# Two graph layers on one core: layer 0's attention with stationary values, two heads in the array's column halves, separate sums spread by transfers, and masks kept in DRAM

## Chip, cores and metric

One core of one Trainium2 chip. The metric is device microseconds of one execution; a kernel's runs here agree within 0.4%. The kernel before takes 5757.45 us (median of 3 runs, 5756.26 to 5758.06).

Ratios are the mean time of one kernel's runs over the mean of the other's runs of the same rounds, with a 95% interval. They are therefore not quite the ratio of the medians quoted.

## The reference, cut to what matters

Eight batches of 2048 nodes with 256 features go through two layers. Layer 0 is attention with four heads of 64 features. Its softmax is taken separately over each chunk of 256 keys, and the eight chunks' results are added:

```python
q, k, v = ...                                     # (B, H=4, N=2048, Dh=64)
kc = k.reshape(B, H, Nc, CHUNK, Dh)               # Nc = 8 chunks of CHUNK = 256 keys
vc = v.reshape(B, H, Nc, CHUNK, Dh)
scores = jnp.einsum('bhnd,bhjcd->bhnjc', q, kc) / jnp.sqrt(Dh)
scores = jnp.clip(scores, -10.0, 10.0)
scores = jnp.where(mask == 0, -10.0, scores)      # mask: the adjacency matrix
attn = jax.nn.softmax(scores, axis=-1)            # within a chunk
ctx = jnp.einsum('bhnjc,bhjcd->bhnd', attn, vc)   # and summed over the chunks
out = layernorm(ctx @ Wo.T + bo + x) * gamma + beta
```

So there are 8 chunks x 4 heads = 32 sums for every query, and a numerator must be divided by its own chunk's sum before it is added to the others. Layer 1 is a graph attention over the same adjacency matrix; the change touches only where it gets its mask.

## The kernel before: what the change and the argument touch

A batch's queries are worked on in four blocks of 512. The logits stand with keys on partitions. The mask is folded into the upper bound of the clip (`bound`, int8, resident in SBUF).

```python
def logits(pool, q, k, p, nb, mt):                # one key tile, two heads
    s = ps_s()
    for i in range(2):
        nc.tensor.matmul(s[:, i, :], k[p][i*DH:(i+1)*DH, mt*P:(mt+1)*P],
                         q[p][i*DH:(i+1)*DH, cols], start=True, stop=True)      # L219
    e = pool.tile([P, 2, NB], F32, tag="e", name="e", bufs=2 * KT)
    nc.vector.scalar_tensor_tensor(e, s, -CLIP * SC, bound[...], op0=ALU.max, op1=ALU.min)   # L224
    nc.scalar.activation(e, e, AF.Exp, scale=1.0 / SC)                          # L228
    return e

def mix(pool, es, ctx4, p, j):                    # one chunk, two heads
    for t2 in range(TB // 2):
        a = ps_a()[:, 0:4 * (DH + 1)].rearrange("p (s d) -> p s d", s=4)
        for s in range(4):
            t, i = 2 * t2 + s // 2, s % 2
            for kt in range(KT):
                nc.tensor.matmul(                                               # L238
                    a[:, s, :], es[kt][:, i, t*P:(t+1)*P], v[:, j*KT+kt, 2*p+i, :],  # v ends in a column of ones
                    start=kt == 0, stop=kt == KT - 1)
        rz = small.tile([P, 4], F32, tag="rz", name="rz")
        nc.vector.reciprocal(rz, a[:, :, DH])                                   # L243
        # DVE: a * rz into ctx4 or part (L248, L251); POOL: ctx4 += part (L252)

for nb in range(NNB):                             # a block
    for p, j in todo:
        es = [logits(...) for kt in range(KT)]
        if ahead is not None: mix(...)            # the chunk before
    ...
    finish_layer0(pool, xs[nb], rns[nb], ctx4)    # transposes L262, projection L271, norm
    start_layer1(xs[nb], nb, sd)                  # norm, transposes L183, projection L300
```

## Time and profile before

The lines that show what bounds this kernel are in the prediction. Layer 0's attention is measured in one batch from the first logits to the last multiplication with values; its tail from there to layer 1's first multiplication (L352).

| kernel before | us |
|---|---|
| one batch (period) | 710.0 |
| attention, 797.9 to 1275.8 | 477.9, of which TensorE busy 468.5 |
| tail, 1275.8 to 1328.5 | 52.7 |
| one block, L300 to L300 | 116.3, of which TensorE busy 110.85 |

The table of windows gives that block as follows. After the window and its length come the busy us (with the number of instructions) of PE, PEld, DVE, ACT and POOL, then the granted TensorE clock, the share of the DMA engines and GB/s.

```profile
1083.30:1199.60 116.30, 110.85 (x690) 82.43 (x690) 66.97 (x139) 40.95 (x45) 32.13 (x37) 0.93 0.00 1
```

### The profile page before, as it was taken

Reading aid. Unit: us, or ns where it says so; the run is one execution under the profiler, and the core shown is the slowest. Engines: PE = TensorE matmul, PEld = TensorE weight load, DVE = VectorE, ACT = ScalarE, POOL = GpSimd, SP = SyncE. Lnnn points to the kernel's source line nnn. Section 1 sums busy time; section 2 is a strip of 40 time slices with the busy share of each in tenths; the row PEclk is TensorE's granted clock in tenths of the full one; section 3 lists DMA queues with packets and bytes.
Section 4 is the critical chain, followed back from the end, with each engine's and each line's share of the span. In section 5 each row is a group of like instructions: output and inputs, shape, how many; then the busy total and the mean of one; then the engine's idle time right before and its main releaser. Section 6 shows DMA issues by size and latency. Waiting matters only on the chain.

```text
span 5753.9 us, 73951 instructions
## 1 busy us (share of the span) xinstructions
PE 5208.2 (91%) x29840; PEld 3939.6 (68%) x29840; DVE 3477.6 (60%) x6501; ACT 2191.4 (38%) x2545; POOL 1228.1 (21%) x1369
## 2 busy tenths in 40 slices
PE   7999799987999889998899978999789997899978
PEld 4777667766677666776667757676576776767767
DVE  4555755558455584555845558455584555845567
ACT  3333443334433344333533335433353333533334
POOL 2222102231022301223112221123211232112221
PEclk7999899999999899998999989999899988999889
DMA  4000000000000000000000000000000000000000
GB/s 150 1 1 1 15 15 1 1 1 15 15 1 1 1 15 15 1 1 1 19 11 1 1 1 23 8 1 1 1 23 8 1 1 1 23 4 1 1 1 15
DMA packets 39203, 57.16 MB, mean 10 GB/s; under 512 B 2000, under 2 KB 36816, under 8 KB 36816
## 3 DMA queue, kind: packets, MB, share of 16 engines
q1 hardware_dynamic: 38864, 52.44, 2.8%
q8 instruction: 238, 3.90, 0.3%
q14 instruction: 101, 0.83, 0.0%
HBM read 35.65 MB, written 16.78 MB: 9 GB/s over the span
## 4 chain that ended last, share of the span: by engine, by line
PE 74%; DVE 14%; POOL 6%; ACT 4%; issue 2%; DMA 0%; POOLq 0%; SPq 0%; ACTq 0%; DVEq 0%
PE ps_a L238 32%; PE ps_s L219 17%; PE ps_a L352 10%; PE ps_m L194 4%; DVE d L328 3%; PE ps_m L300 3%; DVE e L343 2%; DVE st L331 2%; PE ps_m L203 2%; PE ps_m L183 2%; PE ps_s L346 2%; POOL o L282 1%; DVE e L224 1%; PE ps_m L271 1%; ACT e L341 1%
## 5 line engine op out<-in xcount | busy, mean ns | idle before, releaser
L238 PEld LDWEIGHTS ps_a<-v,e 128*128 128x128 f32 x16384 | 1994.8, 202 | 357.8 <-issue 321.4
L238 PE MATMUL ps_a<-v,e 128*128 128x65 f32 x16384 | 2061.0, 287 | 0.0
L228 ACT ACTIVATE e<-e 128x1024 f32<-128x1024 f32 x1024 | 1081.8, 1056 | 1682.4 <-DVE e L224 1650.2
L224 DVE SCALAR_TENSOR_TENSOR e<-ps_s,bound 128x1024 f32<-128x1024 f32 x1024 | 1213.4, 1217 | 273.4 <-PE ps_s L219 273.2
L219 PE MATMUL ps_s<-q,k 64*128 64x512 f32 x4096 | 1211.3, 638 | 66.3 <-DVE e L224 66.3
L252 POOL TENSOR_TENSOR ctx<-ctx,part 128x256 f32<-128x256 f32 x896 | 648.0, 723 | 2698.9 <-DVE part L251 2698.9
L352 PE MATMUL ps_a<-g,eT 128*128 128x257 f32 x4096 | 952.9, 385 | 66.9 <-ACT eT L348 45.9
L352 PEld LDWEIGHTS ps_a<-g,eT 128*128 128x128 f32 x4096 | 756.7, 190 | 214.0 <-ACT eT L348 83.5
L219 PEld LDWEIGHTS ps_s<-q,k 64*128 64x128 f32 x4096 | 389.6, 190 | 391.2 <-issue 148.8
L243 DVE RECIPROCAL rz<-ps_a 128x4 f32<-128x4 f32 x1024 | 182.7, 180 | 783.3 <-PE ps_a L238 783.3
L346 PE MATMUL ps_s<-ident,e 128*128 128x128 f32 x2048 | 288.0, 282 | 180.7 <-DVE e L343 179.8
L251 DVE TENSOR_TENSOR part<-ps_a,rz 128x256 f32<-128x256 f32 x896 | 379.6, 424 | 88.5 <-DVE rz L243 1.4
L360 POOL TENSOR_TENSOR x<-x,r 128x256 f32<-128x256 f32 x128 | 136.3, 1065 | 1254.8 <-DVE st L332 511.9
L346 PEld LDWEIGHTS ps_s<-ident,e 128*128 128x128 f32 x2048 | 247.4, 145 | 221.7 <-DVE e L343 114.4
L348 ACT ACTIVATE eT<-ps_s 128x512 f32<-128x512 f32 x256 | 150.6, 590 | 615.8 <-PE ps_s L346 575.2
L343 DVE TENSOR_TENSOR e<-e,e 128x1024 f32<-128x1024 f32 x256 | 310.1, 1217 | 79.3 <-ACT e L342 79.3
L341 ACT ACTIVATE e<-d,st 128x1024 f32<-128x1024 f32 x256 | 291.2, 1137 | 112.8 <-DVE st L334 112.8
L328 DVE SCALAR_TENSOR_TENSOR d<-sign,dst 128x2048 f32<-128x2048 int8 x128 | 312.7, 2448 | 9.6 <-ACT dst L324 9.6
L342 ACT ACTIVATE e<-d,st 128x1024 f32<-128x1024 f32 x256 | 291.1, 1137 | 0.0
L331 DVE TENSOR_REDUCE st<-d 128x1 f32<-128x2048 f32 x128 | 290.5, 2274 | 0.0
L183 PE MATMUL ps_m<-ident,hn 128*128 128x128 f32 x512 | 121.0, 368 | 165.7 <-ACT hn L173 165.2
L183 PEld LDWEIGHTS ps_m<-ident,hn 128*128 128x128 f32 x512 | 67.2, 175 | 288.8 <-ACT hn L173 237.5
(71 smaller groups left out, 3130.3 us busy)
## 6 DMA issues: line engine op xcount, KB each, us to landing
rows<-in_adj_dram SPq DMA_DIRECT2D x16, 1024.0 KB, 5.0
x<-in_x_dram SPq DMA_DIRECT2D x32, 512.0 KB, 3.8
out_dram<-x SPq DMA_DIRECT2D x32, 512.0 KB, 2.9
raw<-in_L_gnn_Wq_dram SPq DMA_DIRECT2D x1, 256.0 KB, 4.7
raw<-in_L_gnn_Wk_dram SPq DMA_DIRECT2D x1, 256.0 KB, 4.9
raw<-in_L_gnn_Wv_dram SPq DMA_DIRECT2D x1, 256.0 KB, 5.3
raw<-in_L_gnn_Wo_dram SPq DMA_DIRECT2D x1, 256.0 KB, 5.1
w1s<-in_L_gnn_W_dram SPq DMA_DIRECT2D x1, 256.0 KB, 6.4
```

Source lines behind the costliest of these rows:

```text
L219: nc.tensor.matmul(s[:, i, :], k[p][i * DH:(i + 1) * DH, mt * P:(mt + 1) * P], q[p][i * DH:(i + 1) * DH, cols], start=True, stop=True,)
L224: nc.vector.scalar_tensor_tensor(e, s, -CLIP * SC, bound[:, mt, cols][:, None, :].to_broadcast([P, 2, NB]), op0=ALU.max, op1=ALU.min,)
L228: nc.scalar.activation(e, e, AF.Exp, scale=1.0 / SC)
L238: nc.tensor.matmul(a[:, s, :], es[kt][:, i, t * P:(t + 1) * P], v[:, j * KT + kt, 2 * p + i, :], start=kt == 0, stop=kt == KT - 1,)
L251: nc.vector.tensor_tensor(part, num, rzb, op=ALU.mult)
L252: nc.gpsimd.tensor_tensor(dst, dst, part, op=ALU.add)
L328: nc.vector.scalar_tensor_tensor(d, sign[:, t, :], BIG, dst, op0=ALU.mult, op1=ALU.min)
L331: nc.vector.tensor_reduce(dmax, d, AX.X, ALU.max)
L341: nc.scalar.activation(e1, d[:, cols], AF.Exp, bias=b1)
L343: nc.vector.tensor_tensor(e1, e1, e2, op=ALU.max)
L346: nc.tensor.transpose(pt[:, k * P:(k + 1) * P], e1[:, k * P:(k + 1) * P], ident)
L352: nc.tensor.matmul(acc, eT[:, k * P:(k + 1) * P], g[:, m, :], start=m == 0, stop=m == NT - 1)
```

## The change

The intent is to take load and passes off TensorE. Instead of the exponentials, the values are stationary (64 columns), and the exponentials stream in 512 columns. Two heads then use the two column halves of the array. The result now stands with features on partitions, so a sum per query can't be applied as a scalar per partition. The sums come from matmuls of their own against a tile of ones (`picks`, four heads in four column quarters), are inverted once per half block, written to DRAM and spread over 64 partitions per head by broadcasting transfers. The unnormalised numerators wait for that in SBUF tiles `au` of 8 KB per partition, for which room is made by moving both masks to DRAM. The finish of a block is put inside the next block's loop.

```diff
-    bound = const.tile([P, NT, N], I8, name="bound")
-    sign = const.tile([P, NT, N], I8, name="sign")
-    v = const.tile([P, NT, HEADS, DH + 1], F32, name="v")
+    bounds = [dram.tile([P, NT, NB], I8, name=f"bound{i}") for i in range(NNB)]
+    signs = [dram.tile([P, N], I8, name=f"sign{i}") for i in range(NT)]
+    v = const.tile([P, NT, HEADS, DH], F32, name="v")
+    picks = const.tile([P, HALF_J, 32], F32, name="picks")     # ones in JR of 32 columns per chunk
...
+    def mix(es, acc, z, au, mt):
+        j, kt = mt // KT, mt % KT
+        jj = j % HALF_J
+        for p in range(HEADS // 2):
+            for i in range(2):
+                nc.tensor.matmul(                                                  # L254
+                    acc[p][i * DH:(i + 1) * DH, :], v[:, mt, 2 * p + i, :], es[p][:, i, :],
+                    start=kt == 0, stop=kt == KT - 1)
+        for h in range(HEADS):
+            nc.tensor.matmul(                                                      # L259
+                z[32 * h:32 * h + 32, :], picks[:, jj, :], es[h // 2][:, h % 2, :],
+                start=jj == 0 and kt == 0, stop=jj == HALF_J - 1 and kt == KT - 1)
+        if kt == KT - 1:
+            for p in range(HEADS // 2):
+                nc.scalar.activation(au[p][:, jj, :], acc[p], AF.Copy)             # L265
+
+    def normalize(pool, z, au, ctxT, first):                                       # per half block
+        nc.scalar.activation(zc, z, AF.Copy)                                       # L270
+        nc.sync.dma_start(zd, zc[::JR, :])                                         # L275
+        nc.sync.dma_start(zr, zd.rearrange("r (c f) -> (r c) f", c=C))
+        nc.vector.reciprocal(zr, zr)                                               # L277
+        nc.sync.dma_start(rd.rearrange("r (c f) -> (r c) f", c=C), zr)
+        for p in range(HEADS // 2):
+            rb = pool.tile([P, HALF_J, NB], F32, tag="rb", name="rb", bufs=2)
+            for i in range(2):
+                nc.sync.dma_start(rb[i*DH:(i+1)*DH]..., src.partition_broadcast(DH))   # L285
+            a = au[p]
+            nc.vector.tensor_tensor(a, a, rb, op=ALU.mult)                         # L290
+            nc.gpsimd.tensor_tensor(a[:, 0:2, :], a[:, 0:2, :], a[:, 2:4, :], op=ALU.add)  # L291
+            # one more add into ctxT (first half, L293) or two (second half, L295, L296)
...
+                        if m % (KT * HALF_J) == 0:
+                            au = [pool.tile([P, HALF_J, NB], F32, tag="au", name="au", bufs=3)
+                                  for _ in range(HEADS // 2)]
...
+                    if mt == 6 and late:
+                        late.pop()()              # the block before: finish_layer0, start_layer1
```

Left out: the writing and loading of the masks, the projection that now reads `ctxT` without a transpose, removed comments, and one x buffer fewer.

More of the change, by code (lines that the diff above doesn't have):

```diff
@@ L58, in gnn_two_layers @@
     KT = CHUNK // P
+    HALF_J = NCH // 2
+    JR = 32 // HALF_J
     SC = float(DH) ** 0.5
@@ L62, in gnn_two_layers @@
     const = ctx.enter_context(tc.tile_pool(name="const", bufs=1))
-    xpool = ctx.enter_context(tc.tile_pool(name="xpool", bufs=NNB + 1))
+    dram = ctx.enter_context(tc.tile_pool(name="dram", bufs=1, space=bass.MemoryType.DRAM))
+    xpool = ctx.enter_context(tc.tile_pool(name="xpool", bufs=NNB))
     work = ctx.enter_context(tc.tile_pool(name="work", bufs=2))
@@ L107, in gnn_two_layers @@
     w1s = const.tile([P, FC, F], F32, name="w1s")
-    bound = const.tile([P, NT, N], I8, name="bound")
-    sign = const.tile([P, NT, N], I8, name="sign")
-    v = const.tile([P, NT, HEADS, DH + 1], F32, name="v")
+    bounds = [dram.tile([P, NT, NB], I8, name=f"bound{i}") for i in range(NNB)]
+    signs = [dram.tile([P, N], I8, name=f"sign{i}") for i in range(NT)]
+    v = const.tile([P, NT, HEADS, DH], F32, name="v")
     g = const.tile([P, NT, F + 1], F32, name="g")
-    nc.gpsimd.memset(v[:, :, :, DH:DH + 1], 1.0)
     nc.gpsimd.memset(g[:, :, F:F + 1], 1.0)
+    picks = const.tile([P, HALF_J, 32], F32, name="picks")
+    nc.gpsimd.memset(picks, 0.0)
+    for j in range(HALF_J):
+        nc.gpsimd.memset(picks[:, j, j * JR:(j + 1) * JR], 1.0)
     with tc.tile_pool(name="setup", bufs=2) as setup:
@@ L134, in gnn_two_layers @@
             nc.vector.tensor_scalar(z, rows, 0.0, -2.0, op0=ALU.is_equal, op1=ALU.mult)
-            nc.gpsimd.tensor_scalar(sign[:, t, :], z, 1.0, 1.0, op0=ALU.mult, op1=ALU.add)
+            sg = setup.tile([P, N], I8, tag="sg", name="sg")
+            nc.gpsimd.tensor_scalar(sg, z, 1.0, 1.0, op0=ALU.mult, op1=ALU.add)
+            nc.sync.dma_start(signs[t], sg)
+            if t % TB == 0:
+                bd = setup.tile([P, NT, NB], I8, tag="bd", name="bd")
             for half in range(NT // 8):
@@ L140, in gnn_two_layers @@
                     nc.tensor.transpose(pt[:, k, :], z[:, m * P:(m + 1) * P], ident_b)
-                dst = bound[:, half * 8:(half + 1) * 8, t * P:(t + 1) * P]
+                dst = bd[:, half * 8:(half + 1) * 8, t % TB * P:(t % TB + 1) * P]
                 if half % 2 == 0:
@@ L145, in gnn_two_layers @@
                     nc.scalar.activation(dst, pt, AF.Copy, bias=CLIP * SC, scale=CLIP * SC)
+            if t % TB == TB - 1:
+                nc.sync.dma_start(bounds[t // TB], bd)
     nc.sync.dma_start(w1s, w1.rearrange("(c p) f -> p c f", p=P))
@@ L212, in project_qkv, with logits @@
                 )
-    def logits(pool, q, k, p, nb, mt):
+    def logits(pool, q, k, bd, p, nb, mt):
         cols = slice(nb * NB, (nb + 1) * NB)
@@ L222, in logits @@
             )
-        e = pool.tile([P, 2, NB], F32, tag="e", name="e", bufs=2 * KT)
+        e = pool.tile([P, 2, NB], F32, tag="e", name="e", bufs=5)
         nc.vector.scalar_tensor_tensor(
-            e, s, -CLIP * SC, bound[:, mt, cols][:, None, :].to_broadcast([P, 2, NB]),
+            e, s, -CLIP * SC, bd[:, mt, :][:, None, :].to_broadcast([P, 2, NB]),
             op0=ALU.max, op1=ALU.min,
@@ L229, in logits @@
         return e
-    def mix(pool, es, ctx4, p, j):
-        for t2 in range(TB // 2):
-            a = ps_a()[:, 0:4 * (DH + 1)].rearrange("p (s d) -> p s d", s=4)
-            for s in range(4):
-                t, i = 2 * t2 + s // 2, s % 2
-                for kt in range(KT):
-                    nc.tensor.matmul(
-                        a[:, s, :], es[kt][:, i, t * P:(t + 1) * P], v[:, j * KT + kt, 2 * p + i, :],
-                        start=kt == 0, stop=kt == KT - 1,
-                    )
-            rz = small.tile([P, 4], F32, tag="rz", name="rz")
-            nc.vector.reciprocal(rz, a[:, :, DH])
-            dst = ctx4[:, 2 * t2:2 * t2 + 2, 2 * p:2 * p + 2, :]
-            num = a[:, :, 0:DH].rearrange("p (t i) d -> p t i d", t=2)
-            rzb = rz.rearrange("p (t i) -> p t i", t=2)[:, :, :, None].to_broadcast([P, 2, 2, DH])
-            if j == 0:
-                nc.vector.tensor_tensor(dst, num, rzb, op=ALU.mult)
-            else:
-                part = pool.tile([P, 2, 2, DH], F32, tag="part", name="part", bufs=2)
-                nc.vector.tensor_tensor(part, num, rzb, op=ALU.mult)
-                nc.gpsimd.tensor_tensor(dst, dst, part, op=ALU.add)
@@ L254, in finish_layer0 @@
-    def finish_layer0(pool, x4, rn0, ctx4):
-        o4 = pool.tile([P, TB, F], F32, tag="ctx", name="o4", bufs=2)
-        for t2 in range(TB // 2):
-            pt = ps_m()
-            for i in range(2):
-                for c in range(FC):
-                    k = i * FC + c
-                    nc.tensor.transpose(
-                        pt[:, k * P:(k + 1) * P],
-                        ctx4[:, 2 * t2 + i, 2 * c:2 * c + 2, :].rearrange("p h d -> p (h d)"), ident,
-                    )
-            cT = work.tile([P, 2 * FC, P], F32, tag="cT", name="cT")
-            nc.scalar.activation(cT.rearrange("p k n -> p (k n)"), pt, AF.Copy)
+    def mix(es, acc, z, au, mt):
[5 more added lines that the diff above has]
+                    acc[p][i * DH:(i + 1) * DH, :], v[:, mt, 2 * p + i, :], es[p][:, i, :],
+                    start=kt == 0, stop=kt == KT - 1,
+                )
+        for h in range(HEADS):
+            nc.tensor.matmul(
+                z[32 * h:32 * h + 32, :], picks[:, jj, :], es[h // 2][:, h % 2, :],
+                start=jj == 0 and kt == 0, stop=jj == HALF_J - 1 and kt == KT - 1,
+            )
+        if kt == KT - 1:
+            for p in range(HEADS // 2):
+                nc.scalar.activation(au[p][:, jj, :], acc[p], AF.Copy)
@@ new lines, in normalize @@
+    def normalize(pool, z, au, ctxT, first):
+        zc = pool.tile([P, NB], F32, tag="zc", name="zc", bufs=1)
+        nc.scalar.activation(zc, z, AF.Copy)
+        rows = HEADS * HALF_J
+        C = P // rows
+        zr = pool.tile([P, NB // C], F32, tag="zr", name="zr", bufs=2)
+        zd = dram.tile([rows, NB], F32, tag="zd", name="zd", bufs=2)
+        nc.sync.dma_start(zd, zc[::JR, :])
+        nc.sync.dma_start(zr, zd.rearrange("r (c f) -> (r c) f", c=C))
+        nc.vector.reciprocal(zr, zr)
+        rd = dram.tile([rows, NB], F32, tag="rd", name="rd", bufs=2)
+        nc.sync.dma_start(rd.rearrange("r (c f) -> (r c) f", c=C), zr)
+        for p in range(HEADS // 2):
+            rb = pool.tile([P, HALF_J, NB], F32, tag="rb", name="rb", bufs=2)
+            for i in range(2):
+                h = 2 * p + i
+                src = rd[h * HALF_J:(h + 1) * HALF_J, :].rearrange("j n -> (j n)")
+                nc.sync.dma_start(
+                    rb[i * DH:(i + 1) * DH].rearrange("p j n -> p (j n)"),
+                    src.partition_broadcast(DH),
+                )
+            a = au[p]
+            nc.vector.tensor_tensor(a, a, rb, op=ALU.mult)
+            nc.gpsimd.tensor_tensor(a[:, 0:2, :], a[:, 0:2, :], a[:, 2:4, :], op=ALU.add)
+            if first:
+                nc.gpsimd.tensor_tensor(ctxT[:, p, :], a[:, 0, :], a[:, 1, :], op=ALU.add)
+            else:
+                nc.gpsimd.tensor_tensor(a[:, 0, :], a[:, 0, :], a[:, 1, :], op=ALU.add)
+                nc.gpsimd.tensor_tensor(ctxT[:, p, :], ctxT[:, p, :], a[:, 0, :], op=ALU.add)
@@ L268, in finish_layer0 @@
+    def finish_layer0(pool, x4, rn0, ctxT):
+        o4 = pool.tile([P, TB, F], F32, tag="o4", name="o4", bufs=1)
+        for t2 in range(TB // 2):
             pp = ps_m()
             for i in range(2):
+                t = 2 * t2 + i
                 for c in range(FC):
                     nc.tensor.matmul(
-                        pp[:, i * F:(i + 1) * F], cT[:, i * FC + c, :], woT[:, c, :],
+                        pp[:, i * F:(i + 1) * F], ctxT[:, c, t * P:(t + 1) * P], woT[:, c, :],
                         start=c == 0, stop=c == FC - 1,
@@ L326, in layer1 @@
             src = sd[:, 0, t:t + 1]
+            sg = pool.tile([P, N], I8, tag="sg", name="sg", bufs=3)
+            nc.sync.dma_start(sg, signs[t])
             d = pool.tile([P, N], F32, tag="d", name="d", bufs=2)
-            nc.vector.scalar_tensor_tensor(d, sign[:, t, :], BIG, dst, op0=ALU.mult, op1=ALU.min)
+            nc.vector.scalar_tensor_tensor(d, sg, BIG, dst, op0=ALU.mult, op1=ALU.min)
             st = small.tile([P, 5], F32, tag="st", name="st")
@@ L379, in gnn_two_layers, with finish @@
                 rns.append(rn)
+            late = []
             for nb in range(NNB):
-                ctx4 = pool.tile([P, TB, HEADS, DH], F32, tag="ctx", name="ctx4", bufs=2)
-                todo = [(p, j) for p in range(HEADS // 2) for j in range(NCH)]
+                bd = pool.tile([P, NT, NB], I8, tag="bd", name="bd", bufs=2)
+                nc.sync.dma_start(bd, bounds[nb])
+                ctxT = pool.tile([P, FC, NB], F32, tag="ctxT", name="ctxT", bufs=2)
                 ahead = None
-                for p, j in todo:
-                    es = [logits(pool, q, k, p, nb, j * KT + kt) for kt in range(KT)]
+                for mt in range(NT + 1):
+                    if mt < NT:
+                        es = [logits(pool, q, k, bd, p, nb, mt) for p in range(HEADS // 2)]
                     if ahead is not None:
-                        mix(pool, ahead[2], ctx4, *ahead[:2])
-                    ahead = (p, j, es)
-                mix(pool, ahead[2], ctx4, *ahead[:2])
-                finish_layer0(pool, xs[nb], rns[nb], ctx4)
-                start_layer1(xs[nb], nb, sd)
+                        m = mt - 1
+                        half = m // (KT * HALF_J)
+                        if m % (KT * HALF_J) == 0:
+                            z = ps_m()
+                            au = [
+                                pool.tile([P, HALF_J, NB], F32, tag="au", name="au", bufs=3)
+                                for _ in range(HEADS // 2)
+                            ]
+                        if m % KT == 0:
+                            acc = [ps_a() for _ in range(HEADS // 2)]
+                        mix(ahead, acc, z, au, m)
+                        if m % (KT * HALF_J) == KT * HALF_J - 1:
+                            normalize(pool, z, au, ctxT, half == 0)
+                    ahead = es
+                    if mt == 6 and late:
+                        late.pop()()
+                def finish(nb=nb, ctxT=ctxT):
+                    finish_layer0(pool, xs[nb], rns[nb], ctxT)
+                    start_layer1(xs[nb], nb, sd)
+                late.append(finish)
+            late.pop()()
         with tc.tile_pool(name="l1", bufs=1, reuse_waits="tile") as pool:
```

## The prediction

> **What bounds the kernel now.** I read the busy table, the chain that ended last, the costliest groups, then the timeline of PE alone in three windows, a table of windows, and the transfers.
>
> ```profile
> PE 5208.2 (91%) x29840; PEld 3939.6 (68%) x29840; DVE 3477.6 (60%) x6501; ACT 2191.4 (38%) x2545; POOL 1228.1 (21%) x1369
> ...
> PE ps_a L238 32%; PE ps_s L219 17%; PE ps_a L352 10%; PE ps_m L194 4%; DVE d L328 3%; PE ps_m L300 3%; DVE e L343 2%; DVE st L331 2%; PE ps_m L203 2%; PE ps_m L183 2%; PE ps_s L346 2%; POOL o L282 1%; DVE e L224 1%; PE ps_m L271 1%; ACT e L341 1%
> ...
> L238 PEld LDWEIGHTS ps_a<-v,e 128*128 128x128 f32 x16384 | 1994.8, 202 | 357.8 <-issue 321.4
> L238 PE MATMUL ps_a<-v,e 128*128 128x65 f32 x16384 | 2061.0, 287 | 0.0
> ```
>
> TensorE bounds it. The two lines of layer 0's attention, L238 (exponentials times values) and L219 (logits), hold 49% of the chain. In L238 the exponentials are stationary: each pass loads 128x128 weights and streams only 65 columns, so loading costs about as much as multiplying (1995 against 2061 us). The second view, PE's timeline in steady state, gives the unit cost:
>
> ```profile
> 1000.15 1.99 PE L219 MATMUL ps_s<-q,k 64*128 64x512 f32 x8
> 1002.06 3.79 PE L238 MATMUL ps_a<-v,e 128*128 128x65 f32 x32
> 1005.78 1.99 PE L219 MATMUL ps_s<-q,k 64*128 64x512 f32 x8
> ...
> 80.89 3.60 PE L194 MATMUL ps_m<-hT,wkT 128*128 128x512 f32 x8
> ...
> 89.73 1.12 PE L219 MATMUL ps_s<-q,k 64*128 64x512 f32 x2
> ```
>
> From start to start, the unit is 1.91 us of L219 and 3.72 of L238: 5.63 us. A batch has 4 blocks x 16 units. A float32 matmul is recorded as two passes. Eight full-array passes of 512 columns (L194) take 3.44 us from start to start, so one takes 0.43. Eight passes of L219, which use half of the array's rows each, take 1.91, or 4 x 0.43 + 0.19: two heads run at once. A lone head's two passes last 1.12. This is the fact on which the change builds, though for rows, not columns.
>
> Third, what surrounds the loop. A block takes 116.3 us (from one L300 to the next, 1083.3 to 1199.6), of which 16 x 5.63 = 90.1 is loop. Of the other 26.2, about 9.3 is TensorE's own finishing work (L262, L271, L183, L300); the rest is stalls and a slow clock:
>
> ```profile
> 1060.86 1.13 PE L219 MATMUL ps_s<-q,k 64*128 64x512 f32 x4 [1.76 <-DVE e L224]
> 1061.92 6.88 PE L238 MATMUL ps_a<-v,e 128*128 128x65 f32 x32
> ...
> 1061.00:1085.00 24.00, 23.99 (x88) 17.98 (x89) 10.41 (x25) 7.68 (x10) 9.61 (x8) 0.52 0.01 1
> ```
>
> After a gap of 1.76 us the same 32 passes take 6.88 instead of 3.79. The last row is the stretch that follows: PE is busy throughout and the granted clock is 0.52 (the column after POOL). It recovers only in the dense full-array L300, in this and the neighbouring blocks.
>
> Last, the end of layer 0: after the last L238 (1275.8) TensorE has little to do until layer 1's first L352 (1328.5), about 53 us in each batch, a serial chain through DVE, POOL and ACT.
>
> **What the Trainium skill says.** (1) "TensorE: Matmul & The Clock Gate", section "Part 3: Packing small matmuls — row/col tiling": matmuls in different tiles of the array run at once; three column tiles at 512 columns gave 2.38x. The trace agrees for row tiles (8 passes in 1.91 us instead of 3.44); it has no column tiles. (2) "TensorEngine Tiling (Array Packing)", "Key Properties": changing the tiling mode drains the array. The trace allows that: 0.19 us are left over in each L219 group, which I call switch and start. (3) The first page, "Part 1: The HAM clock gate": half clock after at least one idle window of about 3.4 us, full clock after one busy window. The trace differs: 1.76 us idle was enough, and 24 busy us at half clock did not bring it back. (4) "DMA: Bandwidth & Descriptors", "Anatomy of one DMA": a fixed cost of about 2.0 us. The transfer view agrees: 1 KB lands in 2.1 us.
>
> ```profile
> x<-in_x_dram SPq DMA_DIRECT2D x32, 512.0 KB, 3.8
> bq_c<-in_L_gnn_bq_dram SPq DMA_DIRECT2D x1, 1.0 KB, 2.1
> ```
>
> **The change, part by part.** All numbers per unit (one key tile, four heads) or per batch.
>
> *Values stationary (L254).* 4 matmuls, 8 passes of 512 columns, two heads in opposite column halves. If the halves run at once as the rows do: 4 x 0.43 + 0.1 = 1.82 us in place of 3.72.
>
> *Own sums (L259).* 4 more matmuls, 8 passes, in four column quarters. If all four run at once: 2 x 0.43 + 0.1 = 0.96. L219's successor (L233) stays 1.92. The unit becomes 1.92 + 1.82 + 0.96 = **4.70 us** against 5.63, so 64 x 0.93 = **59.5 us less per batch**. The other engines fit: DVE 2 x 1.22 for the clip plus about 5 us of normalising per 8 units, about 3.06 us; ACT 2 x 1.06 plus 0.59 of copying and a little, about 2.8. TensorE stays the bound.
>
> *Normalising through DRAM.* Per half block: copy of the sums 0.6 (ACT), three small transfers of about 2.2 with a short reciprocal, then two broadcasts per head pair, 1 MB, about 5.0 (the 1 MB loads of the adjacency land in 5.0), DVE multiply over 2048 columns 2.4, POOL adds 2.35 + 1.25 (and 1.25 again in the second half). The first pair's buffer is free some 20 to 21 us after the last sum, ACT's copy included. It is needed, since there are three buffers for two per half, when the third unit of the next half starts its second pair: the accumulator's copy waits for the buffer, and the matmul for the copy. In the program's order I count about 17 us of TensorE work up to there at the start of a block and 19.4 in its middle, where the previous block's finish (L197, L335) is put in. So about 4 us of stall at a block's start; in the middle none from this, but some 6.5 us because the transposes L197 come about 11 us of TensorE work after L306, while the DVE-POOL-ACT chain between them takes about 17.
>
> *Block extras.* Before 26.2. After: 8.2 for finishing, 1.9 for pairs that the order breaks up, 1.2 for the empty pipeline at a block's start, 4 + 6.5 of stalls, and 4 for the slow clock after them: 25.8. Nothing won. For the slow clock I choose a short stay, since the new loop streams 512 columns almost without a break, like the lines that ended it before.
>
> *Tail.* The last block has no next one to hide behind. Before, the context was transposed 3.5 us after the last L238. After, the second pair's sum is ready about 25 us after the last matmul, less some 2 for the transposes removed: **+23 us per batch**.
>
> *Masks.* Bounds (1 MB per block) and signs (256 KB per tile, three buffers, land in under 4 us while a tile of layer 1 takes 10) are loaded well ahead: 0. One x buffer fewer: the last block's x is reloaded while the other three are projected: 0.
>
> *Sum.* -59.5 + 0 + 23 = -36.5 per batch, times 8 = -292: 5757 - 292 = **5465 us**.
>
> **Rivals.** *A. Column tiles don't overlap for float32.* For: the trace shows only row tiles; rows of different tiles read different partitions, while column tiles read the same 128 partitions several times over. Against: the skill's measured column tiling. All 16 passes one by one would be 6.9 us, a unit of 8.8, and 3.2 us more than now in each of 512: with the tail about 7550. If only two of the four quarters overlap, the sums cost 0.86 more: +440, about 5900. *B. The stalls eat the gain.* For: a 1.76 us gap cost 24 us at half clock. If every half block trips it and the new loop doesn't recover either, that is about 10 us lost twice per block, 16 more per block than I count: about +510, 5975. Against: denser streaming. *C. The DRAM round trip is longer than I think.* Each 5 us more falls on the tail and on every block start: +25 per batch, +200: 5670. *D. It goes better:* the stalls vanish in the slack and the clock stays up: -12 per block, about 5100.
>
> **Range and chances.** I give column overlap 0.8. Within that, C and part of B leave a spread of about 130 us around 5465, with a tail to 5700. Without it the kernel is slower or even. Range 5240 to 5870. Faster by over 2% 0.73, within 2% 0.11, slower 0.16.
>
> **What would show it.** Right: L254's eight passes in about 1.8 us and L259's in about 1.0, a unit near 4.7; LDWEIGHTS no longer near MATMUL in cost; the chain still on PE, with more DMA, DVE and POOL at the end of each batch; about 75 us between a batch's last L259 and layer 1's first matmul. Wrong: passes of L254 at 0.43 each without overlap (A); PE waiting for ACT's copy of the accumulator, and ACT for POOL, for over 8 us per half block, with the clock at 0.5 for most of a block (B, C).

## The result, and the profile after

The kernel after takes **5994.7 us** (median of 4 runs, 5986.5 to 6001.8), the kernel before in the same rounds 5756.85. The ratio is 1.0413 (1.0398 to 1.0428): slower by 4.1%, where 5465 was predicted.

The top of the page of the kernel after answers to the prediction's first fence:

```profile
PE 4841.2 (81%) x21392; PEld 2273.5 (38%) x21392; DVE 3201.1 (53%) x4645; ACT 2422.3 (40%) x3057; POOL 1238.2 (21%) x797
...
PE 54%; DVE 18%; POOL 13%; DMA 7%; ACT 5%; issue 2%; SPq 0%; POOLq 0%; DVEq 0%; ACTq 0%
...
L254 PE MATMUL ps_a<-e,v 128*64 128x512 f32 x4096 | 1152.6, 660 | 248.5 <-ACT au L265 248.5
L254 PEld LDWEIGHTS ps_a<-e,v 128*64 128x64 f32 x4096 | 266.2, 145 | 992.2 <-issue 640.0
```

TensorE is busy 367 us less, and the weight loads of the multiplication with values fell from 1995 to 266 us. Yet the kernel is longer: the chain that ended last spends 54% on PE instead of 74%, and POOL and DMA, 6% and 0% before, now hold 13% and 7%. The last column of L254 names a new wait, 248.5 us for ACT's copy L265.

TensorE's timeline in steady state answers to the prediction's second fence:

```profile
1044.45 1.99 PE L233 MATMUL ps_s<-q,k 64*128 64x512 f32 x8
1046.37 1.94 PE L254 MATMUL ps_a<-e,v 128*64 128x512 f32 x8
1048.23 1.06 PE L259 MATMUL ps_m<-e,picks 128*32 128x512 f32 x8
1049.23 1.56 PE L233 MATMUL ps_s<-q,k 64*128 64x512 f32 x6
```

From start to start, the unit takes 1.92 + 1.86 + 1.00 = 4.78 us instead of 5.63. The passes of the two column halves start 7 ns apart in the trace. So the mechanism that the change builds on works, at the size predicted.

The time is lost around the unit. These are the same stretches in both kernels (attention from 840.3 to 1320.9 and tail from 1321.0 to 1398.9 in the kernel after):

| one batch | before | after | difference |
|---|---|---|---|
| attention | 477.9 | 480.6 | +2.7 |
| of this TensorE busy | 468.5 | 420.5 | -48.0 |
| of this TensorE idle | 9.4 | 60.1 | +50.7 |
| tail | 52.7 | 77.9 | +25.2 |

Eight times (2.7 + 25.2), and 17 us more before the first projection (75.6 to 92.3 us from the start), make 240 us; measured are 238. The saving in the loop was real, and was turned into waiting.

The table of windows, for one block of the kernel after (L335 to L335):

```profile
1038.70:1158.30 119.60, 100.45 (x425) 30.68 (x424) 57.91 (x81) 48.16 (x61) 32.82 (x19) 0.87 0.20 46
```

Sixteen units of 4.78 are 76.5 us, so 43.1 us are extras; 25.8 were predicted. In this block TensorE is idle for 19.15 us instead of 5.45, and the granted clock has fallen from 0.93 to 0.87. Its waits are these lines of its timeline, and one of 0.53 us at 1086.17; in brackets is the idle time and what ended it:

```profile
1056.77 1.98 PE L254 MATMUL ps_a<-e,v 128*64 128x512 f32 x4 [3.56 <-ACT au L265]
...
1102.88 1.18 PE L233 MATMUL ps_s<-q,k 64*128 64x512 f32 x4 [2.89 <-DVE e L238]
...
1109.49 1.98 PE L254 MATMUL ps_a<-e,v 128*64 128x512 f32 x4 [5.42 <-ACT au L265]
...
1148.32 2.07 PE L233 MATMUL ps_s<-q,k 64*128 64x512 f32 x2 [6.60 <-DVE e L238]
```

Two kinds of wait stand here: L254 for ACT's copy into `au` (twice per block), and L233 for DVE's clip (6.60 us, where the previous block's finish is, and 2.89, where DVE stands at a multiply that waits for its broadcast). What ACT waits for is in the view of the waits (us in total, times, longest):

```profile
ACT au L265 <- POOL ctxT L293: 108.7, 32, 3.7
ACT au L265 <- POOL ctxT L296: 108.3, 24, 4.9
```

ACT waits for POOL's last add, which frees an `au` tile for the next half block. This is the ring of three buffers for two tiles per half. The timeline of all engines shows one turn of it, from the copy of the sums to the multiplication that waits:

```profile
1083.79 0.60 ACT L270 ACTIVATE zc<-ps_m 128x512 f32<-128x512 f32 x1 [0.42 <-PE ps_m L259]
...
1089.13 0.33 SPq L279 DMA_DIRECT2D rd<-zr  x1
...
1092.01 2.37 SPq L285 DMA_DIRECT2D rb<-rd  x4
...
1099.40 2.29 DVE L290 TENSOR_TENSOR au<-au,rb 128x2048 f32<-128x2048 f32 x1 [4.57 <-DMA rb<-rd]
...
1104.27 1.27 POOL L295 TENSOR_TENSOR au<-au 128x512 f32<-128x512 f32 x1
1105.32 2.37 DVE L290 TENSOR_TENSOR au<-au,rb 128x2048 f32<-128x2048 f32 x1
1105.62 3.19 POOL L296 TENSOR_TENSOR ctxT<-ctxT,au 128x512 f32<-128x512 f32 x1
...
1108.84 0.60 ACT L265 ACTIVATE au<-ps_a 128x512 f32<-128x512 f32 x1 [4.92 <-POOL ctxT L296]
```

Between the first two lines the sums go out to DRAM and back (from 1084.42) and the reciprocal runs (1088.56, 0.54 us); POOL's first add, L291, runs from 1101.84 for 2.35 us. The turn takes 25.7 us, from 1083.79 to TensorE's 1109.49. TensorE's work meanwhile is 25.7 - 0.53 - 2.89 - 5.42 = 16.9 us. This turn is one of the longer ones: the hop of the reciprocals to DRAM took 2.9 us, where the median of 64 such hops is 1.45. The median of the 32 turns at a block's start is 24.2 us, and that of the 24 in a block's middle 35.2.

The clock follows these gaps. The trace's clock records put it at one half from 1056.05 to 1062.87 (at the gap of 3.56 us), from 1103.83 to 1114.07 (after that of 2.89 and through that of 5.42) and from 1144.79 to 1158.44 (in that of 6.60), and at full for the rest of the block but its first 0.28 us. TensorE is busy for 21.0 us of this time at half clock.

### The profile page after: what moved, and what is told of

It is laid out like the page before. It is cut to its first block, busy times and chain, and to the rows that moved or that the text cites. A ratio compares the mean times of both kernels' runs of the same rounds, so it can differ in the third digit from the quotient of the medians.

```text
span 5993.0 us, 54681 instructions
## 1 busy us (share of the span) xinstructions
PE 4841.2 (81%) x21392; PEld 2273.5 (38%) x21392; DVE 3201.1 (53%) x4645; ACT 2422.3 (40%) x3057; POOL 1238.2 (21%) x797
## 4 chain that ended last, share of the span: by engine, by line
PE 54%; DVE 18%; POOL 13%; DMA 7%; ACT 5%; issue 2%; SPq 0%; POOLq 0%; DVEq 0%; ACTq 0%
PE ps_a L254 13%; PE ps_s L233 12%; PE ps_a L389 10%; PE ps_m L259 6%; DMA rb<-rd 4%; PE ps_m L208 4%; DVE e L238 3%; DVE d L365 3%; POOL au L291 3%; DVE au L290 2%; PE ps_m L335 2%; DVE e L380 2%; DVE st L368 2%; PE ps_m L306 2%; PE ps_m L217 2%
## 5 line engine op out<-in xcount | busy, mean ns | idle before, releaser
L238 DVE SCALAR_TENSOR_TENSOR e<-ps_s,bd 128x1024 f32<-128x1024 f32 x1024 | 1215.8, 1218 | 1198.0 <-PE ps_s L233 1088.5
L233 PE MATMUL ps_s<-q,k 64*128 64x512 f32 x4096 | 1216.6, 653 | 216.7 <-DVE e L238 216.6
L254 PE MATMUL ps_a<-e,v 128*64 128x512 f32 x4096 | 1152.6, 660 | 248.5 <-ACT au L265 248.5
L291 POOL TENSOR_TENSOR au<-au 128x1024 f32<-128x1024 f32 x128 | 300.9, 2351 | 2524.7 <-DVE au L290 2429.3
L233 PEld LDWEIGHTS ps_s<-q,k 64*128 64x128 f32 x4096 | 389.8, 195 | 962.4 <-issue 619.2
L254 PEld LDWEIGHTS ps_a<-e,v 128*64 128x64 f32 x4096 | 266.2, 145 | 992.2 <-issue 640.0
L259 PE MATMUL ps_m<-e,picks 128*32 128x512 f32 x4096 | 598.3, 620 | 0.0
L265 ACT ACTIVATE au<-ps_a 128x512 f32<-128x512 f32 x512 | 297.3, 587 | 380.0 <-PE ps_a L254 162.9
L290 DVE TENSOR_TENSOR au<-au,rb 128x2048 f32<-128x2048 f32 x128 | 306.4, 2393 | 188.0 <-DMA rb<-rd 169.9
L187 ACT ACTIVATE hn<-x,krn 128x256 f32<-128x256 f32 x256 | 139.4, 592 | 493.7 <-POOL o L317 322.9
L306 PE MATMUL ps_m<-woT,ctxT 128*128 128x256 f32 x512 | 153.1, 451 | 207.1 <-POOL ctxT L296 207.1
L365 DVE SCALAR_TENSOR_TENSOR d<-sg,dst 128x2048 f32<-128x2048 int8 x128 | 312.8, 2449 | 9.6 <-ACT dst L359 9.6
```

Of the source, the lines that this page charges most:

```text
L233: nc.tensor.matmul(s[:, i, :], k[p][i * DH:(i + 1) * DH, mt * P:(mt + 1) * P], q[p][i * DH:(i + 1) * DH, cols], start=True, stop=True,)
L238: nc.vector.scalar_tensor_tensor(e, s, -CLIP * SC, bd[:, mt, :][:, None, :].to_broadcast([P, 2, NB]), op0=ALU.max, op1=ALU.min,)
L254: nc.tensor.matmul(acc[p][i * DH:(i + 1) * DH, :], v[:, mt, 2 * p + i, :], es[p][:, i, :], start=kt == 0, stop=kt == KT - 1,)
L259: nc.tensor.matmul(z[32 * h:32 * h + 32, :], picks[:, jj, :], es[h // 2][:, h % 2, :], start=jj == 0 and kt == 0, stop=jj == HALF_J - 1 an ...
L265: nc.scalar.activation(au[p][:, jj, :], acc[p], AF.Copy)
L290: nc.vector.tensor_tensor(a, a, rb, op=ALU.mult)
```

## The experiments

Two theories were left by the profile, and they don't exclude each other. **The ring:** three `au` tiles are too few for a round trip of 25.7 us beside 17 us of work, which makes two gaps per block and, through them, a slow clock. **The finish:** the in-order DVE stands at the statistics of the previous block's finish while the clip waits behind them, which makes the gap of 6.6 us. Rivals: the round trip through DRAM is the whole cost, whatever the buffers; the masks' transfers cost time; the column halves overlap worse than the unit suggests. In the expectations of the first runs, the waits of the ring and for the reciprocals are "theory W", and the finish is "rival F".

| run | median us | ratio to before (95%) |
|---|---|---|
| after | 5994.7 | 1.0413 (1.0398 to 1.0428) |
| e1_au4: fourth `au` tile | 5559.81 | 0.9657 (0.9643 to 0.9672) |
| e1_nodma: no round trip, result wrong | 5585.84 | 0.9702 (0.9687 to 0.9716) |
| e1_late11: finish later | 5947.22 | 1.0329 (1.0314 to 1.0344) |
| e1_masks: before, masks in DRAM | 5775.72 | 1.0032 (1.0015 to 1.0049) |
| e2_room3: e1_au4's room, three tiles | 5995.44 | 1.0407 (1.0389 to 1.0426) |
| e2_split: e1_au4, finish in two pieces | 5404.27 | 0.9387 (0.9373 to 0.9401) |
| e2_order: e1_au4, halves not alternating | 5588.08 | 0.9708 (0.9694 to 0.9723) |
| e2_au4nodma: fourth tile and no round trip, result wrong | 5587.56 | 0.9702 (0.9686 to 0.9718) |
| e3_split13: second piece still later | 5407.91 | 0.9398 (0.9381 to 0.9415) |
| e3_split3: e2_split, three tiles | 5862.75 | 1.0189 (1.0173 to 1.0205) |
| e3_tail: e2_split, last half without transfers | 5376.42 | 0.9340 (0.9325 to 0.9355) |
| e3_both: e3_tail and e3_split13 | 5374.26 | 0.9335 (0.9319 to 0.9352) |

All results agree with the reference, except in the two runs that are wrong on purpose.

### A fourth tile (e1_au4), and its control (e2_room3)

SBUF had no room for a fourth tile. Three edits that leave the work alone make it; the fourth line is the experiment. The control has the first three alone.

```diff
-    ident_b = const.tile([P, P], BF16, name="ident_b")        # moved to the setup pool
-    picks = const.tile([P, HALF_J, 32], F32, name="picks")
+    picks = const.tile([P, 64 - JR], F32, name="picks")       # one window that slides over the ones
-        zr = pool.tile([P, NB // C], F32, tag="zr", name="zr", bufs=2)
+        zr = pool.tile([P, NB // C], F32, tag="zr", name="zr", bufs=1)
-    pool.tile([P, HALF_J, NB], F32, tag="au", name="au", bufs=3)
+    pool.tile([P, HALF_J, NB], F32, tag="au", name="au", bufs=4)
```

> The changed kernel with a fourth buffer for the unnormalised sums (room made by moving a setup tile, a narrower selector and one zr buffer). Theory W (the gain is given back to waits on the DRAM round trip of the reciprocals: ACT's copy waits for POOL to free one of three buffers, and DVE stands in order behind the broadcast): ACT's waits for POOL (217 us in the trace after) go, TensorE's 248 us of waits for that copy go, DVE's wait for the broadcast stays: 5750 to 5850 us. Rival F (the previous block's finish, put into the middle of the block, costs it): under 60 us gained, above 5930.

> Control: the room made for the fourth buffer (setup tile moved, narrower selector, one zr buffer) but still three buffers. If the ring of three is the cause, this stays at 5980 to 6010 us. If the layout or the schedule that came with it were the cause, it goes to about 5560.

Measured: 5559.81 us with four tiles, 5995.44 with three and the same room. The control stands where the kernel after stands, so the fourth tile alone is worth 436 us, 7.3% of the kernel. TensorE's timeline of e1_au4 over one block has lost the waits of the multiplication with values (L253 in this file); only three waits for DVE's clip are left, 6.60, 0.53 and 0.78 us. The run is 190 us faster than the expectation's 5750, which kept DVE's wait for the broadcast as a cost. That wait is still there (169.9 us in all in the kernel after, 189.6 here), but in the blocks shown TensorE loses 0.78 us to it instead of 2.89.

Its block, in the table of windows:

```profile
959.30:965.90 6.60, 0.01 (x2) 0.00 (x0) 2.77 (x9) 0.20 (x2) 3.72 (x2) 0.66 0.04 10
965.90:979.50 13.60, 13.44 (x35) 6.19 (x36) 5.12 (x14) 6.43 (x10) 1.02 (x1) 0.66 0.25 60
979.50:1060.90 81.40, 80.08 (x390) 23.39 (x388) 49.83 (x60) 41.56 (x52) 28.21 (x17) 1.00 0.24 57
```

The block takes 101.6 us, and the prediction's block was 75.2 + 25.8 = 101.0 (by another sum, as told below). After the finish the clock is 1.00 to the block's end. TensorE's busy time fell from 100.45 to 93.53 us for the same work (425 and 426 records), and its idle time from 19.15 to 8.07. So of the 18.0 us between the two blocks, 11.1 were waiting. Of the other 6.9, about 6.0 are the slower clock: TensorE was busy at half clock for 21.0 us and is for 9.0 now, and half of the difference is lost time (an estimate). The ring theory is shown.

### No round trip (e1_nodma, e2_au4nodma)

The same with three tiles, but the multiply takes a constant tile, and the transfers and the reciprocal go. The result is wrong on purpose (relative error 0.81). The second kernel has four tiles as well.

```diff
-        nc.sync.dma_start(zd, zc[::JR, :])
-        ...                                                   # zr, reciprocal, rd, rb
-            nc.vector.tensor_tensor(a, a, rb, op=ALU.mult)
+            nc.vector.tensor_tensor(a, a, flat, op=ALU.mult)
```

> The changed kernel without the transfers and the reciprocal: sums are still made and copied out, but the multiply takes a constant (wrong result on purpose). Theory W: both waits go and the tail is some 16 us shorter in each batch; a block takes about 101 us instead of 119.6: near 5300 us. Rival F: only the tail shortens, near 5865.

> Four buffers and no transfers of the reciprocals (wrong result on purpose). If with four buffers the round trip is hidden everywhere but at a batch's end: about 16 us less in each of 8 batches, 5430 us. If the broadcasts still disturb the loop: under 5350.

Measured: 5585.84 and 5587.56 us, far above the 5300 of theory W and the 5430 of the second expectation. With a short turn three tiles suffice: the waits for ACT's copy are gone here too, and a fourth tile adds nothing. This is the second way to the same end, and it says that the turn's length against the ring's depth is what counts, not the transfers as such; the real round trip with four tiles (5559.81) is even 26 us faster than none with three. That last difference is not to be read further. Without the transfers the scheduler orders the block differently, and TensorE gets two gaps per block, 2.59 and about 4 us, which e1_au4 does not have. So e2_au4nodma, meant to show what the round trip costs once the ring is deep enough, doesn't settle that.

### The finish later (e1_late11) and in two pieces (e2_split, e3_split13, e3_split3)

The timeline of DVE and TensorE in the kernel after, at the finish of the previous block, shows the second wait:

```profile
1025.90 0.75 DVE L174 BATCH_NORM_STATS2 stats<-x 128x6 f32<-128x256 f32 x2 [6.20 <-POOL x L325]
...
1028.68 2.07 PE L233 MATMUL ps_s<-q,k 64*128 64x512 f32 x2 [6.61 <-DVE e L238]
```

DVE waits 6.20 us for POOL to finish x, with layer 1's statistics at the head of its queue. The clip that TensorE needs stands behind them, and starts at 1027.43. One remedy is to emit the whole finish later, another to emit layer 1's start apart from it:

```diff
-                    if mt == 6 and late:              # e1_late11: mt == 11
-                        late.pop()()
+                    if mt in (6, 10) and late:        # e2_split, e3_split3; e3_split13: (6, 13)
+                        late.pop(0)()
-                late.append(finish)
+                late.append(lambda nb=nb, ctxT=ctxT: finish_layer0(pool, xs[nb], rns[nb], ctxT))
+                late.append(lambda nb=nb: start_layer1(xs[nb], nb, sd))
```

> The changed kernel with the previous block's finish emitted at unit 11 instead of 6, so away from the half's end. Theory W: the waits for the reciprocals stay, within 60 us of 5995 either way. Rival F: the 6.6 us gap and its slow clock go, about 15 us for each of 24 blocks: near 5650 to 5750.

> Four buffers, and the finish emitted in two pieces, the projection and layer norm at unit 6 and layer 1's start at unit 10. The one gap left in a block is 6.6 us (DVE stands at the statistics of x, which wait for POOL, with the next clip behind it), followed by 13.7 us at half clock. If that order is the cause: some 10 us for each of 24 blocks, 5300 to 5350 us. If another wait takes its place: 5500 or more.

> Four buffers, layer 1's start emitted at unit 13 instead of 10. With unit 10 a gap of 5.4 us was left in each block, DVE at the statistics of x behind three POOL additions of 2.3 us. If more distance removes it: about 6 us for each of 24 blocks, near 5260. If the transposes then wait elsewhere: 5400 or more.

> Three buffers as in the change, with the finish in two pieces (units 6 and 10). If ring and finish cost independently: 156 us less than 5995, so 5840. If the ring's wait is what lasts longest anyway and only moves: 5900 to 5995.

Measured: moving the whole finish gave 47 us (5947.22), with the ring's waits still there. In its trace the wait of 6.6 us is gone, but the transposes L197 wait 8.9 us for ACT's `hn` in its place. Splitting it gave 156 us with four tiles (5559.81 to 5404.27; 5300 to 5350 had been expected) and 133 with three (5995.44 to 5862.75). The two causes are therefore nearly independent, and with three tiles the split does not get below the kernel before. The block of e2_split is 96.3 us, of which all but the first 12.3 run at full clock without a wait:

```profile
937.20:942.60 5.40, 0.03 (x2) 0.00 (x0) 1.54 (x3) 0.00 (x0) 3.74 (x2) 0.69 0.00 0
942.60:949.50 6.90, 6.84 (x26) 2.02 (x28) 4.57 (x14) 5.51 (x8) 1.02 (x1) 0.75 0.04 10
949.50:1033.50 84.00, 83.98 (x400) 26.90 (x396) 51.78 (x67) 42.88 (x53) 28.08 (x17) 1.00 0.28 65
```

The gap of 5.4 us that is left has the same cause: DVE waits for POOL's x with the statistics first in its queue. e3_split13 was to remove it, and missed. The gap stayed at 5.42 us and the time at 5407.91, because the scheduler puts the statistics where it had put them before. Emitting them later in the program does not place them later on DVE; I did not find what would.

### The order of the column halves (e2_order)

```diff
-        for p in range(HEADS // 2):
-            for i in range(2):
+        for i in range(2):
+            for p in range(HEADS // 2):
```

> Four buffers, with the four matmuls of a unit's values in the order left, left, right, right of the array's column halves in place of left, right, left, right. If the halves run at once whatever the order: 5560 us. If TensorE overlaps only neighbours in its queue: 1.86 us a unit become up to 3.5, and 512 of them make up to 6400.

Measured: 5588.08 us, 28 more than e1_au4. With left, left, right, right instead of alternating halves, passes still start in pairs (13 ns apart instead of 7), and L253 and L258 together still take 2.87 us. So the overlap doesn't hang on the order in which the program names the halves. The records don't name the half, so it is not shown that the passes reach the array in that order, and I did not trace the 28 us. Column tiles that don't overlap, rival A, are excluded by the unit in any case.

### The masks alone (e1_masks)

The kernel before, with the masks written to DRAM and loaded as in the change, and nothing else.

```diff
-    bound = const.tile([P, NT, N], I8, name="bound")
-    sign = const.tile([P, NT, N], I8, name="sign")
+    bounds = [dram.tile([P, NT, NB], I8, name=f"bound{i}") for i in range(NNB)]
+    signs = [dram.tile([P, N], I8, name=f"sign{i}") for i in range(NT)]
```

> The kernel before with only the masks moved to DRAM. If the masks cost only setup (first projection 17 us later in the trace after): 5770 to 5780 us. If their loads disturb every batch: 5800 or more.

Measured: 5775.72 us, 17 more than the kernel before in the same rounds (5758.69). The first projection starts at 94.5 us instead of 75.6. The cost is thus paid once, in the setup, and the loads in the batches are hidden. The kernel after pays about the same (75.6 to 92.3).

### The tail (e3_tail, e3_both)

For the last half block of a batch, which has no next block to hide behind, the sums are inverted on DVE straight from PSUM and spread over the partitions by small matmuls, without transfers.

```diff
+    def normalize_last(pool, z, au, ctxT):
+        nc.vector.reciprocal(zc, z)
+        ...
+                        nc.tensor.matmul(sp[i * DH:(i + 1) * DH, k, :],
+                            s4[32 * h:32 * h + 32, jj:jj + 1].to_broadcast([32, DH]),
+                            zc[32 * h:32 * h + 32, :], start=True, stop=True)
+                nc.vector.tensor_tensor(pair, pair, sp, op=ALU.mult)
```

> e2_split with the last half of each batch normalised without transfers: reciprocal on DVE from PSUM, spread by small matmuls, multiply from PSUM, the second pair's additions on DVE. The wait of 18 to 23 us before the output projection should fall to about 12: 11 us for each of 8 batches, near 5315 us. If the reciprocal over 512 columns or the cold array eats it: 5390 or more.

> Unit 13 and the tail without transfers together: the sum of the two, near 5180 us if they are independent.

Measured: 5376.42 us, 28 less than e2_split, a third of what I had hoped for. From the end of the sums to the output projection the tail takes 23.2 us (1170.2 to 1193.5) instead of 26.6 (1174.4 to 1201.0); 3.4 us in each of 8 batches are 27 us. The timeline shows what stands in the way:

```profile
1170.24 3.36 DVE L303 RECIPROCAL zc<-ps_m 128x512 f32<-128x512 f32 x1 [4.18 <-PE ps_m L262]
...
1177.81 5.65 PE L361 MATMUL ps_m<-w1s,hT 128*128 128x256 f32 x16
...
1183.39 4.31 PE L312 MATMUL ps_s<-zc,s 32*64 32x512 f32 x18
```

The reciprocal over 512 columns takes 3.36 us, and the spreading matmuls L312 stand behind layer 1's projection L361 of the block before. e3_both, 5374.26 us, is not to be told from e3_tail and far from the 5180 expected, as e3_split13 had won nothing. Its median is the lowest: 6.6% below the kernel before.

## Why the prediction was wrong, point by point

**Right: what bounds the kernel, and the unit.** L254 took 1.86 us (1.82 predicted), L259 1.00 (0.96), the unit 4.78 (4.70). Per batch that is 64 x 0.85 = 54 us less instead of 59.5.

**Right: the tail.** +25.2 us per batch where +23 was predicted, 77.9 us in all where "about 75" was. Its sum takes off 2 us where the 3.5 us that it names for the kernel before belong, and the second pair's sum came 27.8 us after the last matmul, not 25; the two errors nearly cancel.

**Slightly wrong: the masks.** Put at 0; they cost 17 us once, in the setup, which the prediction did not look at.

**Wrong: "Block extras", and in it the terms for stalls and for the slow clock.** The prediction has "4 + 6.5 of stalls" and "4 for the slow clock after them: 25.8. Nothing won." Measured are 43.1. The ring's wait was named (three buffers for two per half; ACT waits for POOL, TensorE for ACT), but the turn of a buffer was put too short, and the waits of the in-order DVE, at the broadcast and at the statistics, with TensorE's clip behind them, were not in it.

- *The start of a block.* TensorE's work up to the wait was put at 17 us and is 16.9. The turn of the buffer was put at "some 20 to 21 us" and is 25.7. Two terms carry the difference. The broadcasts were put at 5.0 us, from plain 1 MB loads; from the first issue to the multiply it is 1099.40 - 1092.01 = 7.4 us. Four are issued together and land one after the other, 4.8, 7.3, 9.7 and 12.1 us after the first issue (medians of 64 groups), and the multiply needs two. The POOL adds were put at 2.35 + 1.25 + 1.25 and took 7.0 us, because the last one took 3.19. The rest is the hop from the reciprocal to the broadcast, 2.9 us instead of 2.2, longer than usual. TensorE thus stands still for 8.8 us (0.53 + 2.89 + 5.42) instead of 4: 5.42 for the ring, 2.89 behind the broadcast.
- *The slow add.* DVE's multiply L290 of the second pair starts at 1105.32 and ends at 1107.69; POOL's add beside it starts at 1105.62 and ends at 1108.81, that is 1.12 us after DVE. An add alone takes 1.27. So POOL did next to nothing until DVE was done. It is no accident of one line: in this kernel 31 adds L293 and 25 adds L296 set out beside such a multiply; they took 3.18 to 3.35 us and ended 1.12 us after it, and the other 72 took 1.26 to 1.27. The Trainium skill has it, in "SBUF — State Buffer", section "Who interferes with whom": a DVE instruction with two inputs in SBUF and a GpSimd instruction that reads SBUF exclude each other, and the later one is blocked until the other ends. This trace agrees; no run changes this alone. The kernel before gave no sign of it: its DVE multiplies (L251) read one of their inputs from PSUM, and its POOL adds of 128x256 took 0.72 us in the mean. I scaled the add's duration from there and did not ask what its new neighbour reads.
- *The middle of a block.* No stall from the ring was expected; it is 3.56 us. There the reciprocal ran only at 1035.93, some 12 us after its data was requested (1024.06), since the finish's statistics and clips stood ahead of it on DVE. The add that frees the tile was blocked by a multiply as well (3.32 us), and ended at 1056.08, 34 us after the copy of the sums (1021.65). Against this turn stand some 25 us of TensorE's work, part of it at half clock, where the prediction had 20 to 21 against 19.4.
- *The finish.* Its 6.5 us were right in size (6.60), but the wait is another. The prediction has the transposes L197 waiting for the chain; what waits is L233, for the clip behind the statistics. Both hang on POOL's x, so the size is partly luck.
- *The clock.* Five gaps per block instead of the two predicted keep it down longer. By the prediction's parts, idle time should have been about 10.5 + 1.2 = 11.7 us of a block, the rest 89.3 us busy, 4 us of them owed to the clock. Measured are 19.15 idle (+7.5) and 100.45 busy (+11.1). The slower unit accounts for 16 x 0.08 = 1.3 of the latter. Of the 21.0 us that TensorE is busy at half clock, half is lost: about 10.5 us (an estimate), 6.5 more than the 4 counted. Without that loss the block holds 90 us of work, and those of e1_au4 and e2_split, with 9.0 and 3.4 us at half clock, hold 89, so the estimate fits. The last 3.3 us are work that the prediction's parts lack; I did not look where. The "short stay" that I chose was right in kind (6.8 to 13.7 us, where the kernel before stayed for 24 and 17), but it is paid three times per block.

So 7.5 us of waiting, 6.5 of slow clock, 1.3 of the slower unit and 3.3 of other work are the 18.6 us by which the block missed 101.0. The fourth tile brings the block to 101.6, but that this is so near is partly luck: it has 8.1 us idle instead of 11.7, since the ring's stall is gone, and this pays for the work that was missed. What then remains between e1_au4's 5560 and the predicted 5465 is small: attention 54.0 us less per batch instead of 59.5 (44 us in all), the tail 26.7 more instead of 23 (30 us), the setup 17 us. That makes 91 of 95.

**The rivals.** A is excluded. C (a longer round trip) and B (stalls and the clock) were both true, C in part, and stand in series: the longer turn makes the gap, and the gap makes the slow clock. With the fourth tile the ring's gaps go, and with them two of the three stays at half clock. The turn is longer not by the transfers alone, but also by POOL's blocked add and DVE's queue. B's figure of 5975 is near the measured time. I gave the two together too little weight: C and part of B were a spread of 130 us around 5465, and the range ended at 5870.

## What to carry to other kernels

A ring of buffers is sized by the longest time from a buffer's last fill to its release, against the bottleneck engine's work until it is needed again; here turns of some 24 us against 17 us of work, and of 35 against 25, cost 436 us, and one more tile of 8 KB per partition turned +4.1% into -3.4%. When a change moves work onto other engines, take its durations beside its new neighbours, not beside its old ones, and look at what else stands in those engines' queues in program order. A gap in TensorE's work should be booked together with the slow clock that follows it, gap by gap.

## What the Trainium skill lacked or had wrong

- "TensorE: Matmul & The Clock Gate", Part 1: one idle window of about 3.4 us to lose the full clock, one busy window to regain it. The length of the window agrees: of 1039 stays at half clock in the traces of all 14 kernels, 1025 last a whole multiple of 3.41 us. The rest agrees in part. Gaps of 0.53 and 0.78 us left the clock at 1.00, but 1.76 us was enough to halve it in the kernel before, while 1.90 us in e2_order was not. In the block of the kernel after, two stays ended after 6.1 and 4.8 us of TensorE's busy time, the third after 9.8; the kernel before stayed at half clock through 23.9 busy us.
- The same page, Part 3: it has no times for float32, whose matmuls are recorded as two passes. Eight passes of 512 columns took 3.44 us over the full array, 1.86 in two column halves and 1.00 in four column quarters. The order of the halves in the program (alternating or not) left the overlap as it was.
- "DMA: Bandwidth & Descriptors", "Anatomy of one DMA": a fixed 2.0 us and bytes / 436e3, fitted on another issuing path than the one used here. Hops of 32 KB landed in 1.8, 1.7 and 1.5 us, below the fixed cost. That formula is for one transfer alone, and gives an estimate of 3.2 us for 512 KB; of four broadcasts of this size issued together, the first landed 4.8 us after its issue and the last 10.3 (medians of 64; 8.0 over all 256), and in a stretch of them the DMA engines were 98% busy at 205 GB/s.
- "VectorE: DVE Perf Modes": it says how a reciprocal is computed, not how long it takes. Over 128x512 it took 3.36 us, an add of the same shape 0.69.

The views behind the third point, the transfers of the kernel after (size, median us from issue to landing) and a window of it:

```profile
rb<-rd SPq DMA_DIRECT2D x256, 512.0 KB, 8.0
```

```profile
1041.00:1044.00 3.00, 3.00 (x18) 1.34 (x16) 2.29 (x13) 1.02 (x2) 0.00 (x0) 1.00 0.98 205
```
